# Reordering the side work of a chunked linear-attention loop (adaLN block with a mixture of experts, one Trainium2 core)

## The chip, the cores and the metric

The kernel runs on one core of a Trainium2 chip. The metric is device time in microseconds (us), as the median of several runs. The engines are PE (TensorE), DVE (VectorE), ACT (ScalarE) and POOL (GpSimd); SP issues DMAs. All of them run their own instruction streams and wait for one another through semaphores.

## What is computed

An adaLN transformer block on x of shape (4, 2048, 256), all in fp32: causal linear attention with 16 heads of 16, then a router that sends each token to two of eight experts.

```python
mod = (silu(c) @ wmod).reshape(4, 6, 1, -1)
sa, ca, ga, sb, cb, gb = ...            # ga, gb pushed away from zero
h = layernorm(x) * (1 + ca) + sa
q, k, v = phi(h @ wq.T), phi(h @ wk.T), h @ wv.T      # phi(a) = elu(a) + 1
# per head, over t:  S += k_t v_t^T ;  z += k_t
#                    out_t = (S^T q_t) / max(z . q_t, 1e-6)
x = x + ga * (out @ w_out.T)
h = layernorm(x) * (1 + cb) + sb
gates = softmax(h @ w_router.T); top 2; at most 1280 tokens an expert
x = x + gb * sum_e combine_e * (silu(h @ w_gate.T) @ w_down[e].T)
```

## The kernel before

Tokens are taken in groups of G = 512 (16 groups, `g`), and each group in NT = 4 chunks of 128 tokens (`j`). The kernel has three stages: a setup with a preamble for the first groups, the token loop (`for s in range((NG + 2) * NT)`, L743), and the expert stage from L827 on. The expert stage isn't touched by the change.

**One chunk of the token loop.** `scores` (L406) computes the in-chunk scores on PE into the PSUM tile `psc` (one buffer), and DVE masks them in two operations `at` (L419). A chunk later `attend` (L457) multiplies the masked scores with the values into `po`, ACT copies it to `oT` (L472), and `project_out` (L475, through `done()`) multiplies `oT` with the gated output weights `wob`, and DVE adds the result `pw` to x and takes its statistics (L485, L260). `keep_state` (L428) adds the chunk's key-value product `pst` to `s_acc` on DVE, and POOL masks it into `s_msk` (L444); `from_state` (L447) uses that state at the end of the next chunk. So `psc` of a chunk can start only when both `at` of the chunk before are done.

**Side work.** Around this fixed part, each chunk carries pieces of three other groups:

- for the next group (`nxt` = g+1): `project` for k and q (L303: PE, then ACT exp and relu, then one DVE operation), `values` (L319), `keys_by_token` (L338, PE transposes that ACT copies to `kk`), `running_keys` (L352, a DVE scan `zc` for each half h), `times_keys` (L365, the POOL product `zq`), `denominators` (L371: PE sums `zq` into `pd`, DVE computes `den` and `rden`), `scaled_q` (L387: PE spreads `rden` into `pr`, DVE computes `qs`, ACT computes `qeo`);
- for the group after it (`nrm` = g+2): the first layer norm (`stats`, `spread_of`, `normalise` to `xna` on ACT) and `to_features` (transposes `pta` on PE, `hTa` on ACT); the input tile itself is loaded for g+3;
- for groups behind: `prv` = g-1 has its second norm (`xnm`), `to_features` (`ptm`, `hTm`), `logits`, `ranks` (softmax and top 2 on DVE), `row_inputs` (POOL, two products a chunk of rows into `hrow`); `old` = g-2 has `dispatch` (PE positions `pp`, fourteen small DVE operations, the last of them `idx`) and `send` (POOL issues two indirect DMAs for each of the four row tiles, `slots<-hrow,idx`).

**PSUM.** Everything that isn't `psc`, `po` or `pst` goes through `bank()` (L75), a pool of two tiles: the third bank asked for waits until the first was read out.

```python
    ps = ctx.enter_context(tc.tile_pool(name="ps", bufs=2, space=PSUM))
    def bank(name):
        return ps.tile([P, 512], F32, tag="bank", name=name)
```

**What sets the order.** The instructions of PE, ACT and DVE stand in program order (L721); POOL's are placed by a scheduler, which in the steady state puts most of the eight `send` DMAs of a group early in the group.

```python
    with tc.manual_schedule(engines={ET.PE, ET.Activation, ET.DVE}):
```

In one steady group the banks follow each other on PE as: k0, pw(3), k1, q0, pp | q1, pw(0), v0 | pd, v2, pw(1), ptm0, ptm1, pr0, pr1 | pl, kk0, kk2, pw(2), pta0, pta1, lt, with `|` between chunks.

SP's queue holds the loads of x, the zero-fill of the 10,240 row slots (L617, eight DMAs in each of ten early chunks) and the writes of x to the output (L495).

## Time and profile before

| | |
|---|---|
| median of 3 runs | 1087.3 us (1087.07 to 1090.0) |
| the profiled execution | 1088.37 us, its span 1086.7 us |
| token loop, from the first `psc` to the first expert transposes | 67.3 to 759.5 us of the span |
| write of x of groups 0, 1, 2, 3 issued at | 107.0, 144.6, 180.5, 222.1 us |
| the same for groups 4 to 12 | 264.2, 307.4, 349.6, 392.2, 434.4, 477.8, 520.0, 562.7, 605.0 us |
| the same for groups 13, 14, 15 | 648.4, 689.2, 716.8 us |

How to read it: the write of a group's x is issued when its last chunk was added, some 7 us into the next group, so the differences are the group periods. The page of the profile gives busy time and counts for each engine and the costliest groups of instructions, "idle before" being the time its engine stood still ahead of them and what ended that. A line `L419 DVE TENSOR_TENSOR at<-psc,tri ... x128` reads: source line, engine, operation, output from inputs, count. PEld is PE's weight load, which overlaps with PE. PEclk is the granted share of PE's clock.

### The profile page before, as it was taken

To read this page: it belongs to the slowest core of one execution; us is meant where nothing else is said; L and a number is where in the kernel's file an instruction comes from. 1 tells how busy PE (TensorE), PEld (TensorE's weight loads), DVE (VectorE), ACT (ScalarE), POOL (GpSimd) and SP (SyncE) were. 2 spreads that over 40 slices of the span, in tenths; PEclk is the share of its full clock that TensorE was granted. 3 is DMA by queue.
4 is the path that set the end of the run, shared out by engine and by line. 5 is a ranking of instruction groups with operands and counts; after the bars stand their busy time and mean duration, and the time that the engine had idled before them with its cause. 6 is when DMAs were issued, how large, how long until landed. Compare 5 with 4: busy or idle time off the path is not lost.

```text
span 1086.7 us, 17841 instructions
## 1 busy us (share of the span) xinstructions
PE 915.0 (84%) x6832; PEld 642.5 (59%) x6832; DVE 626.7 (58%) x1448; ACT 363.2 (33%) x722; POOL 563.1 (52%) x690
## 2 busy tenths in 40 slices
PE   5879989879779888897897798740999999999996
PEld 4547756656656656566565576620566666666664
DVE  3546887676685676676766856742334444434443
ACT  0344534425434344344254343210221221222221
POOL 3122565664844746636638547554535445445553
PEclk9989999899899899899899999955999999999998
DMA  5006766221221212202201100022544444344321
GB/s 193 1 1 235 266 227 245 99 99 40 100 72 68 99 50 70 93 35 66 75 33 51 37 30 14 29 78 68 198 138 137 142 162 147 125 160 161 112 68 49
DMA packets 62901, 110.68 MB, mean 102 GB/s; under 512 B 9934, under 2 KB 30670, under 8 KB 62816
## 3 DMA queue, kind: packets, MB, share of 16 engines
q1 hardware_dynamic: 39040, 59.71, 16.7%
q0 software_dynamic: 17920, 42.48, 11.2%
q10 hardware_dynamic: 5856, 7.35, 2.0%
q8 instruction: 54, 0.88, 0.3%
q14 instruction: 31, 0.25, 0.1%
HBM read 47.69 MB, written 74.68 MB: 113 GB/s over the span
## 4 chain that ended last, share of the span: by engine, by line
PE 49%; issue 14%; POOL 13%; DVE 10%; ACT 7%; DMA 5%; SPq 0%; POOLq 0%; DVEq 0%; ACTq 0%
PE pe L695 9%; POOL slots L625 7%; PE ph L681 7%; PE pk L310 5%; DMA rows<-slots 4%; PE pv L325 4%; PE pw L484 3%; PE psc L413 3%; PE po L464 3%; PE pst L434 3%; PE pr L395 3%; PE pq L310 2%; POOL zq L369 2%; PE po L452 1%; POOL s_msk L444 1%
## 5 line engine op out<-in xcount | busy, mean ns | idle before, releaser
L625 POOL DMA_INDIRECT slots<-hrow,idx x128 | 144.5, 1129 | 68.3 <-DVE idx L610 28.4
L695 PE MATMUL pe<-wd,hid 128*128 128x256 f32 x640 | 158.9, 385 | 11.6 <-DVE hid L690 8.7
L419 DVE TENSOR_TENSOR at<-psc,tri 128x1024 f32<-128x1024 f32 x128 | 150.0, 1213 | 23.4 <-PE psc L413 23.3
L681 PE MATMUL ph<-hTe,wg_sb 128*128 128x512 f32 (+1 forms) x384 | 153.3, 526 | 0.7 <-issue 0.7
L695 PEld LDWEIGHTS pe<-wd,hid 128*128 128x128 f32 x640 | 116.0, 189 | 56.5 <-DVE y L702 14.7
L707 POOL DMA_INDIRECT out_dram<-y,tok x80 | 78.6, 982 | 98.0 <-DVE y L706 54.6
L659 POOL DMA_INDIRECT xc<-out_dram,tok x80 | 81.2, 1015 | 68.7 <-issue 44.3
L689 ACT ACTIVATE th<-ph 128x512 f32<-128x512 f32 (+1 forms) x96 | 50.5, 526 | 190.8 <-PE ph L681 134.2
L681 PEld LDWEIGHTS ph<-hTe,wg_sb 128*128 128x128 f32 x384 | 70.6, 191 | 45.0 <-issue 31.8
L690 DVE SCALAR_TENSOR_TENSOR hid<-th,ph 128x512 f32<-128x512 f32 (+1 forms) x96 | 57.0, 596 | 62.4 <-ACT th L689 46.3
L702 DVE SCALAR_TENSOR_TENSOR y<-pe,rows 128x256 f32<-128x256 f32 x80 | 38.6, 483 | 87.4 <-PE pe L695 58.7
L413 PE MATMUL psc<-qeo,k 32*128 32x256 f32 x1024 | 74.3, 404 | 16.0 <-DVE at L419 16.0
L325 PE MATMUL pv<-wqkv_sb,hTa 128*128 128x256 f32 x256 | 79.3, 466 | 5.0 <-ACT req L316 4.7
L444 POOL TENSOR_TENSOR s_msk<-s_acc,bd 128x256 f32<-128x256 f32 x60 | 50.6, 843 | 60.5 <-DVE s_acc L442 46.9
L484 PE MATMUL pw<-wob,oT 128*128 128x256 f32 x256 | 71.2, 402 | 5.9 <-ACT kk L350 2.6
L325 PEld LDWEIGHTS pv<-wqkv_sb,hTa 128*128 128x128 f32 x256 | 58.6, 240 | 20.9 <-ACT req L316 11.0
L464 PE MATMUL po<-at,vpad 128*32 128x128 f32 x2048 | 70.6, 278 | 0.2 <-issue 0.2
L484 PEld LDWEIGHTS pw<-wob,oT 128*128 128x128 f32 x256 | 50.0, 202 | 30.5 <-issue 15.7
L485 DVE TENSOR_TENSOR x<-x,pw 128x256 f32<-128x256 f32 x64 | 26.6, 416 | 71.6 <-PE pw L484 71.6
L310 PE MATMUL pk<-hTa,wqkv_sb 128*128 128x512 f32 x128 | 62.9, 617 | 4.8 <-ACT rek L316 4.4
L464 PEld LDWEIGHTS po<-at,vpad 128*32 128x32 f32 x2048 | 52.8, 110 | 21.9 <-issue 21.6
L413 PEld LDWEIGHTS psc<-qeo,k 32*128 32x128 f32 x1024 | 46.7, 186 | 26.9 <-DVE at L419 18.9
(147 smaller groups left out, 1518.5 us busy)
## 6 DMA issues: line engine op xcount, KB each, us to landing
slots<-free SPq DMA_DIRECT2D x80, 262.0 KB
rows<-slots SPq DMA_DIRECT2D x16, 1048.0 KB
x<-in_x_dram SPq DMA_DIRECT2D x16, 512.0 KB
out_dram<-x SPq DMA_DIRECT2D x16, 512.0 KB
rows<-slots SPq DMA_DIRECT2D x8, 524.0 KB
wd<-in_wdT_dram ACTq DMA_DIRECT2D x8, 512.0 KB
slots<-hrow,idx POOLq DMA_INDIRECT x128
wmod_sb<-in_wmod_dram ACTq DMA_DIRECT2D x1, 1536.0 KB
```

Source lines behind the costliest of these rows:

```text
L310: nc.tensor.matmul(pq, wqkv_sb[:, k, o + h * P : o + (h + 1) * P], hT[:, k, :], start=(k == 0), stop=(k == NH - 1))
L325: nc.tensor.matmul(pv[:, i * D : (i + 1) * D], hT[:, k, (j + i) * P : (j + i + 1) * P], wqkv_sb[:, k, 2 * D : 3 * D], start=(k == 0), stop ...
L413: nc.tensor.matmul(psc[:, a, h], kT[r : r + 32, h, cols], qeo[r : r + 32, h, :, cols], start=True, stop=True,)
L419: masked = nc.vector.tensor_tensor(at, psc[:, 2 * m : 2 * m + 2].rearrange("p i h q t -> p (i h q) t"), tri.unsqueeze(1).to_broadcast([P, ...
L444: nc.gpsimd.tensor_tensor(s_msk, s_acc, bd.unsqueeze(1).to_broadcast([P, NH, P]), ALU.mult)
L464: nc.tensor.matmul(po[32 * a : 32 * a + 32, h * P : (h + 1) * P], vp[:, j, h * 4 + a, q : q + 2, :], att[a // 2][:, a % 2, h, q, :], start ...
L484: nc.tensor.matmul(pw[:, :D], oT[:, h, :], G_["wob"][:, h, :], start=(h == 0), stop=(h == NH - 1))
L625: row = nc.gpsimd.indirect_dma_start(out=slots[:, :], out_offset=bass.IndirectOffsetOnAxis(ap=idx[:, c, j : j + 1], axis=0), in_=hr[:, j, ...
L659: got = nc.gpsimd.indirect_dma_start(out=xc[:, i + j, :], out_offset=None, in_=out[:, :], in_offset=bass.IndirectOffsetOnAxis(ap=tok[:, j ...
L681: nc.tensor.matmul(ph[:, :m], wg_sb[:, k, f * P : (f + 1) * P], hT[:, k, :m], start=(k == 0), stop=(k == NH - 1),)
L695: nc.tensor.matmul(pe[:, j, :], hid[:, f, j * P : (j + 1) * P], wds[e][:, f, :], start=(f == 0), stop=(f == NF - 1),)
L707: put = nc.gpsimd.indirect_dma_start(out=out[:, :], out_offset=bass.IndirectOffsetOnAxis(ap=tok[:, j : j + 1], axis=0), in_=y[:, j, :], in ...
```

## The change

The changed kernel does the same operations on the same shapes. Only one kind is added: the routed positions `pp` are copied from PSUM to an SBUF tile `pos` by ACT, and `dispatch` reads `pos`. The rest is moved:

- POOL joins the engines with a fixed order. `send` is issued four DMAs at a time in chunks 2 and 3 (before: in each chunk), `row_inputs` in the same two chunks; `zq` is issued directly after the scan of its half.
- k is projected a group further ahead: in chunk 3 for g+2 (before: in chunk 0 for g+1). The transposes `pta` that it needs move from chunk 3 to chunk 2.
- q stands in chunk 0 (both halves), `keys_by_token` in chunk 1 (before: chunk 3), both `values` in chunk 1, `dispatch` in chunk 1 (before: chunk 0).
- The first norm of g+2 is applied (`xna`) in chunk 0 (before: chunk 2); its statistics are taken a group earlier, for g+3 in chunk 2 (before: for g+2 in chunk 1). The load of g+3 stays in chunk 1.
- `nmr` (shift of the norm) becomes a function of its own, `shift_of`, issued earlier than `normalise`; `wob` has two buffers and is made ahead; the constants of `hrow` are written with row 0.
- The preamble also takes the statistics of group 2 and projects k of group 1.

The banks of a steady group now follow as: q0, pw(3), q1 | kk0, kk2, pw(0), v0, v2, pp | pd, pta0, pta1, pw(1), ptm0, ptm1, pr0, pr1 | pl, k0, pw(2), k1, lt. On ACT, chunks 0 and 1 are: oT(3), exp and relu of q0 and q1, four `xna`, oT(0), two kk copies, four `vpad` copies, four `xnm`, `pos`, oT(1). On DVE, chunk 1 is: two `at`, `s_acc`, x, statistics, scan of half 1, `dispatch`; chunk 2 begins with the next two `at`, `den`, `rden`.

The diff, without context that says nothing:

```diff
@@ -272,12 +272,16 @@
         nc.gpsimd.tensor_tensor(rstd, ve, mhalf, ALU.pow)
         G_["mr", which] = mv, rstd
 
+    def shift_of(g, which):
+        mv, rstd = G_.pop(("mr", which))
+        nmr = small.tile([P, NT], F32, tag=f"nmr{which}", name=f"nmr{which}_{g}")
+        nc.vector.scalar_tensor_tensor(nmr, mv[:, :, 0], -1.0, rstd, ALU.mult, ALU.mult)
+        G_["ns", which] = nmr, rstd
+
     def normalise(g, which, src):
 
         n = f"{which}_{g}"
-        mv, rstd = G_.pop(("mr", which))
-        nmr = small.tile([P, NT], F32, tag=f"nmr{which}", name=f"nmr{n}")
-        nc.vector.scalar_tensor_tensor(nmr, mv[:, :, 0], -1.0, rstd, ALU.mult, ALU.mult)
+        nmr, rstd = G_.pop(("ns", which))
         xn = w1.tile([P, NT, D], F32, tag=f"xn{which}", name=f"xn{n}")
         for j in range(NT):
             nc.scalar.activation(
@@ -349,24 +353,20 @@
                     )
             nc.scalar.copy(kk[:, j : j + 2].rearrange("p j h s -> p (j h s)"), pk)
 
-    def running_keys(g):
+    def running_keys(g, hs):
 
         kT = G_["k", g]
-        zc = w2.tile([P, NH, G], F32, tag="zc", name=f"zc_{g}")
-        for h in range(NH):
+        if 0 in hs:
+            G_["zc", g] = w2.tile([P, NH, G], F32, tag="zc", name=f"zc_{g}")
+            G_["zq", g] = w1.tile([P, NH, G], F32, tag="zq", name=f"zq_{g}")
+        zc = G_["zc", g]
+        for h in hs:
             nc.vector.tensor_tensor_scan(
                 zc[:, h, :], ones_g, kT[:, h, :],
                 0.0 if g % GPB == 0 else G_["zc", g - 1][:, h, G - 1 : G],
                 ALU.mult, ALU.add,
             )
-        G_["zc", g] = zc
-        G_.pop(("zc", g - 1), None)
-
-    def times_keys(g, h):
-
-        if h == 0:
-            G_["zq", g] = w1.tile([P, NH, G], F32, tag="zq", name=f"zq_{g}")
-        nc.gpsimd.tensor_tensor(G_["zq", g][:, h, :], G_["zc", g][:, h, :], G_["q", g][:, h, :], ALU.mult)
+            nc.gpsimd.tensor_tensor(G_["zq", g][:, h, :], zc[:, h, :], G_["q", g][:, h, :], ALU.mult)
 
     def denominators(g):
 
@@ -472,38 +472,33 @@
         nc.scalar.copy(oT.rearrange("p h t -> p (h t)"), po[:, : NH * P])
         G_["oT", g, j] = oT
 
+    def gated_out(b):
+
+        wob = G_["wob", b] = w2.tile([P, NH, D], F32, tag="wob", name=f"wob_{b}")
+        for h in range(NH):
+            nc.gpsimd.tensor_tensor(wob[:, h, :], wout_sb[:, h, :], gab[:, b, 0, :], ALU.mult)
+
     def project_out(g, j):
-        b = g // GPB
-        if g % GPB == 0 and j == 0:
-            wob = G_["wob"] = w1.tile([P, NH, D], F32, tag="wob", name=f"wob_{g}")
-            for h in range(NH):
-                nc.gpsimd.tensor_tensor(wob[:, h, :], wout_sb[:, h, :], gab[:, b, 0, :], ALU.mult)
-        oT, xt = G_.pop(("oT", g, j)), xs[g]
+        wob, oT, xt = G_["wob", g // GPB], G_.pop(("oT", g, j)), xs[g]
         pw = bank(f"pw_{g}_{j}")
         for h in range(NH):
-            nc.tensor.matmul(pw[:, :D], oT[:, h, :], G_["wob"][:, h, :], start=(h == 0), stop=(h == NH - 1))
+            nc.tensor.matmul(pw[:, :D], oT[:, h, :], wob[:, h, :], start=(h == 0), stop=(h == NH - 1))
         nc.vector.tensor_tensor(xt[:, j, :], xt[:, j, :], pw[:, :D], ALU.add)
         stats(g, "m", j, xt)
 
 
     to_slots, added = [], []
 
-    def second_norm(g):
-
-        b = g // GPB
-        xt = xs[g]
-        added.append(nc.sync.dma_start(og[g], xt))
-        hr = hrows[g % 2]
-        if g % GPB < 2:
-            nc.gpsimd.tensor_copy(
-                hr[:, :, O_GB : O_GB + D], gab[:, b, 1, :].unsqueeze(1).to_broadcast([P, NT, D])
-            )
-        nc.gpsimd.tensor_scalar(hr[:, :, O_TOK], tok0, float(g * G), None, ALU.add)
-
     def row_inputs(g, j):
 
-        b = g // GPB
-        h2 = hrows[g % 2][:, j, :D]
+        b, hr = g // GPB, hrows[g % 2]
+        if j == 0:
+            if g % GPB < 2:
+                nc.gpsimd.tensor_copy(
+                    hr[:, :, O_GB : O_GB + D], gab[:, b, 1, :].unsqueeze(1).to_broadcast([P, NT, D])
+                )
+            nc.gpsimd.tensor_scalar(hr[:, :, O_TOK], tok0, float(g * G), None, ALU.add)
+        h2 = hr[:, j, :D]
         nc.gpsimd.tensor_tensor(h2, G_["xm", g][:, j, :], scb[:, b, 1, :], ALU.mult)
         nc.gpsimd.tensor_tensor(h2, h2, scb[:, b, 0, :], ALU.add)
 
@@ -566,21 +561,27 @@
         state["cnt"] = cnt
         G_["route", g] = gt_, mask, rank, cnt
 
-    def dispatch(g):
-
-        gt_, mask, rank, cnt = G_.pop(("route", g))
-        hr = hrows[g % 2]
-
-        def wide(t):
-            return t.unsqueeze(2).to_broadcast([P, NT, NE])
-
-        pp = bank(f"pp_{g}")
+    def positions(g):
+        gt_, mask, rank, cnt = G_["route", g]
+        pp = G_["pp"] = bank(f"pp_{g}")
         nc.tensor.matmul(
             pp[:, : NT * NE], tri, mask.rearrange("p j e -> p (j e)"), start=True, stop=False
         )
         nc.tensor.matmul(
             pp[:, : NT * NE], ones, cnt[:, :NT, :].rearrange("p j e -> p (j e)"), start=False, stop=True
         )
+        pos = small.tile([P, NT * NE], F32, tag="pos", name=f"pos_{g}")
+        nc.scalar.copy(pos, pp[:, : NT * NE])
+        G_["pos"] = pos
+
+    def dispatch(g):
+
+        gt_, mask, rank, cnt = G_.pop(("route", g))
+        hr, pp = hrows[g % 2], G_.pop("pos")
+
+        def wide(t):
+            return t.unsqueeze(2).to_broadcast([P, NT, NE])
+
         flat = gt_.rearrange("p j e -> p (j e)")
 
         slot = small.tile([P, NT, NE], F32, tag="slot", name=f"slot_{g}")
@@ -718,21 +719,24 @@
     NG = N // G
     ET = mybir.EngineType
 
-    with tc.manual_schedule(engines={ET.PE, ET.Activation, ET.DVE}):
-        for g in range(2):
+    with tc.manual_schedule(engines={ET.PE, ET.Activation, ET.DVE, ET.Pool}):
+        gated_out(0)
+        for g in range(3):
+            if g == 1:
+                load_x(2)
             for j in range(NT):
                 stats(g, "a", j, xs[g])
             spread_of(g, "a")
-            normalise(g, "a", xs[g])
-            to_features(g, "a", 0)
+            if g < 2:
+                shift_of(g, "a")
+                normalise(g, "a", xs[g])
+                to_features(g, "a", 0)
+                for h in range(NH):
+                    project(g, "k", h, D, 2)
             if g == 0:
-                load_x(2)
-                for h in range(NH):
-                    project(0, "k", h, D, 2)
-                running_keys(0)
                 for h in range(NH):
                     project(0, "q", h, 0, 1)
-                    times_keys(0, h)
+                running_keys(0, (0, 1))
                 values(0, 0)
                 values(0, 2)
                 denominators(0)
@@ -744,6 +748,7 @@
             g, j = divmod(s, NT)
             nxt = g + 1 if g + 1 < NG else None
             nrm = g + 2 if g + 2 < NG else None
+            far = g + 3 if g + 3 < NG else None
             prv = g - 1 if 0 <= g - 1 < NG else None
             old = g - 2 if g >= 2 else None
 
@@ -751,7 +756,7 @@
                 if last is not None:
                     project_out(*last)
                     if last[1] == NT - 1:
-                        second_norm(last[0])
+                        added.append(nc.sync.dma_start(og[last[0]], xs[last[0]]))
 
             if g < NG:
                 masked = scores(g, j)
@@ -765,60 +770,65 @@
                 logits(prv)
             if g < NG and not (g % GPB == GPB - 1 and j == NT - 1):
                 keep_state(g, j)
+            for i in {2: (0, 1), 3: (2, 3)}.get(j, ()):
+                if old is not None:
+                    send(old, i)
+            for i in {2: (0, 1), 3: (2, 3)}.get(j, ()):
+                if prv is not None:
+                    row_inputs(prv, i)
             if j == 0:
                 if nxt is not None:
-                    project(nxt, "k", 0, D, 2)
+                    project(nxt, "q", 0, 0, 1)
+                done()
+                if prv is not None:
+                    spread_of(prv, "m")
+                if nxt is not None:
+                    project(nxt, "q", 1, 0, 1)
+                    running_keys(nxt, (0,))
+                if nrm is not None:
+                    shift_of(nrm, "a")
+                    normalise(nrm, "a", xs[nrm])
+                if prv is not None:
+                    shift_of(prv, "m")
+            elif j == 1:
+                if nxt is not None:
+                    keys_by_token(nxt)
                 done()
                 if nxt is not None:
-                    project(nxt, "k", 1, D, 2)
-                    project(nxt, "q", 0, 0, 1)
-                if prv is not None:
-                    spread_of(prv, "m")
-                if old is not None:
-                    dispatch(old)
-                if nxt is not None:
-                    running_keys(nxt)
-                    times_keys(nxt, 0)
-            elif j == 1:
-                if nxt is not None:
-                    project(nxt, "q", 1, 0, 1)
-                    times_keys(nxt, 1)
+                    running_keys(nxt, (1,))
+                    values(nxt, 0)
+                    values(nxt, 2)
                 if prv is not None:
                     normalise(prv, "m", xs[prv])
                     G_["xm", prv] = G_["xnm", prv]
-                done()
-                if nxt is not None:
-                    values(nxt, 0)
+                    xs.pop(prv)
+                if old is not None:
+                    positions(old)
+                    dispatch(old)
+                if far is not None:
+                    load_x(far)
+            elif j == 2:
                 if nrm is not None:
-                    for i in range(NT):
-                        stats(nrm, "a", i, xs[nrm])
-                    spread_of(nrm, "a")
-                if g + 3 < NG:
-                    load_x(g + 3)
-            elif j == 2:
-                if nxt is not None:
-                    values(nxt, 2)
+                    to_features(nrm, "a", 0)
                 done()
                 if prv is not None:
                     to_features(prv, "m", 2)
-                if nrm is not None:
-                    normalise(nrm, "a", xs[nrm])
                 if nxt is not None:
                     scaled_q(nxt)
+                if far is not None:
+                    for i in range(NT):
+                        stats(far, "a", i, xs[far])
+                    spread_of(far, "a")
             else:
-                if nxt is not None:
-                    keys_by_token(nxt)
+                if nrm is not None:
+                    project(nrm, "k", 0, D, 2)
                 done()
                 if nrm is not None:
-                    to_features(nrm, "a", 0)
+                    project(nrm, "k", 1, D, 2)
+                if g % GPB == GPB - 1 and g + 1 < NG:
+                    gated_out(g // GPB + 1)
                 if prv is not None:
                     ranks(prv)
-                    xs.pop(prv)
-            if old is not None:
-                send(old, j)
-            if prv is not None and j >= 1:
-                for i in {1: (0,), 2: (1, 2), 3: (3,)}[j]:
-                    row_inputs(prv, i)
             last = None
             if g < NG:
                 from_state(g, j)
```

## The prediction

> **What bounds the kernel now.** I read the page first (engine totals, slices), then the waits, then one steady group in the timeline, then stretches of it with the granted clock.
>
> ```profile
> PE 915.0 (84%) x6832; PEld 642.5 (59%) x6832; DVE 626.7 (58%) x1448; ACT 363.2 (33%) x722; POOL 563.1 (52%) x690
> ...
> PEclk9989999899899899899899999955999999999998
> ```
>
> PE is the busiest engine, but in the token loop the clock line dips once a group. The waits name the stall behind it:
>
> ```profile
> PEld pd L377 <- POOL zq L369: 51.7, 14, 4.2
> PE pd L377 <- POOL zq L369: 47.9, 14, 3.9
> ```
>
> The timeline of group 7 shows its cause and cost:
>
> ```profile
> 357.19 2.33 DVE L357 TENSOR_TENSOR_SCAN zc<-ones_g,k 128x512 f32<-128x512 f32 x2
> ...
> 365.13 0.97 POOL L625 DMA_INDIRECT slots<-hrow,idx  x1 [0.30 <-issue]
> ...
> 366.79 1.29 POOL L369 TENSOR_TENSOR zq<-zc,q 128x512 f32<-128x512 f32 x1
> ...
> 368.14 0.65 PE L377 MATMUL pd<-zq,hpick 128*32 128x128 f32 x8 [3.94 <-POOL zq L369]
> ...
> 369.74 3.62 PE L325 MATMUL pv<-wqkv_sb,hTa 128*128 128x256 f32 x8
> ```
>
> The second `zq` stands behind four sends on POOL; PE waits 3.94 us, and afterwards runs cold: the `pv` that takes 1.83 us from start to next start in chunk 1 (358.56 to 360.39) takes 3.41 here (369.74 to 373.15). The stretches agree:
>
> ```profile
> 364.00:368.10 4.10, 0.20 (x8) 0.00 (x0) 3.57 (x10) 1.77 (x5) 3.77 (x4) 0.87 0.70 205
> 368.10:371.50 3.40, 3.36 (x17) 2.62 (x18) 1.58 (x3) 0.00 (x0) 3.23 (x5) 0.50 0.58 224
> 371.50:374.90 3.40, 3.40 (x13) 2.66 (x11) 0.32 (x1) 0.65 (x2) 3.21 (x4) 0.65 0.14 55
> ```
>
> Groups 3 to 12 take (605.0 - 180.5)/10 = 42.45 us each; groups 1 and 2, without the stall and at clock 1.00, 37.6 and 35.9. Half clock lasts 3.4 and 6.8 us in turn, which costs half of that, 2.56 us on average. So before is 36 us of work, some 3.9 of stall, some 2.6 of cold clock. DVE is busy 29.7 us of such a group (stretch 307.4 to 349.6), so it has little slack once PE no longer stalls.
>
> **What the Trainium skill says.** "TensorE: Matmul & The Clock Gate", Part 1: PE drops to half clock after an idle window of about 3.4 us, windows run free, and a busy window restores it. The trace agrees (0.50 above) and is stricter: going through its windows, one with PE idle for 57% of it was already followed by half clock. A stall of some 2 us or more can therefore trigger it. The same page, "Architectural detail", calls ACT and DVE strict FIFOs; the trace agrees: at 362.81 `xnm` runs its 2.08 us on ACT while `pv`, done at 360.39, waits behind it for its copies. "Perfetto Trace Analysis", Optimizing Tensor Performance, asks that matmul groups rotate through PSUM banks so that the evacuation of one hides under the next; with two banks, a third group waits for the first one's reader, and that is where the new order gets into trouble.
>
> **The change part by part.** *The `zq` wait.* `zq` now follows its scan on POOL (1.29 us) and comes a chunk before `pd`. The 3.9 us stall and its cold clock go: up to 6.4 us a group.
>
> *What is late next.* I laid one group of the new order out with durations from the timeline above, warm clock, taking A = start of the first `at` on DVE. Each step is the latest of what it waits for:
>
> 1. DVE chunk 0: two `at` 2.26, `s_acc` 0.35, q0 0.6, x 0.45, statistics 0.43, aggregates 0.41, `ve` 0.25, q1 0.6, scan 1.1, `nmra` 0.4: A+6.85.
> 2. ACT has the four `xna` ahead of oT(0) and kk. They need `nmra`: 2.08, then oT 0.37, kk 0.55: A+9.85. `pw`(0) needs oT(0) and the bank of kk0, so PE stands there. PE itself got there at A+6.6 (the next psc starts 4.85 before A; +1.08, attend 1.02, pst 0.55, q 1.75, pw 0.86, q1 1.98 with its wait, po 0.45, psc 1.08, attend 1.02, pst 0.55, kk 1.1). First new stall: 3.25 us.
> 3. PE `pw` 0.86, v0 1.73, v2 1.73: A+14.2.
> 4. ACT v copies 0.65, `xnm` 2.08 (moved ahead of it), `pos` 0.2: A+17.1. `pos` isn't in the trace; the 128x32 ACT row of gates is 0.23. Bounds 0.15 to 0.3.
> 5. DVE has been free since A+12.75 and can't go past `dispatch`: 4.35 us of wait. Dispatch 2.98, the next two `at` 2.3, `den` 0.3: A+22.7. Queued behind it are these `at`, and PE's chunk.
> 6. PE went on (pp 0.35, po 0.45, psc, attend, pd 0.4, pst, pta0 0.55) to A+18.65; `pta1` needs the bank of `pd`, which `den` frees. Second new stall: 4.1 us.
> 7. PE pta1 0.55, pw 0.86, ptm 1.1 and pr 1.8 with 0.35 of waiting for ACT: A+27.35. (DVE's qs, the statistics of g+3 and the `at` end at A+32.3, not last.)
> 8. PE po 0.45, psc 1.08, attend 1.02, pl 0.5, pst 0.6, k0 1.72: A+32.7; ACT exp and relu 1.08, PE k1 1.75, ACT 1.1: A+36.7.
> 9. DVE k1 0.68, ranks 3.7 (342.32 to 346.04): next A at A+41.05.
>
> A cold clock comes on top. Where the window boundaries fall decides: after the first stall the loss on steps 3 is 0 to 3 us, after the second 1.4 to 3 us on step 7. Followed through successive groups it settles near 1.7 + 1.6, a period of 13 windows (44.4 us; before is 12.5 windows). So a steady group goes from 42.45 to 44.4, +1.95.
>
> *Other groups.* Group 2 already has dispatch and late ranks in it: 35.9 to some 44, +8. Group 1: no dispatch, PE-bound, -1.5. Group 13 lacks the statistics of g+3: -1. Group 14 lacks `xna`, `pta` and the k projection: 40.8 to some 33, -8. Group 15 loses a POOL wait (4.55 us of PE at 710.58 for `s_msk` behind sends) as POOL's fixed order puts `s_msk` first: -4.
>
> *Preamble.* k of group 1 (two cold projections, exp, relu, DVE) and the statistics of group 2 now stand before the first psc, +5.5; the first group has that much less to wait for, +4 net.
>
> *Drain.* Sends of group 14 start after `xnm` 2.08, `pos` and dispatch instead of before: the first at 4.5 us after the last x addition (716.32 to 720.87), now some 8; POOL is serial from there: +3.5.
>
> *At nothing:* `wob` ahead (8 x 0.73 on POOL, busy 25 of 42 us), `shift_of` (same instruction; its `rstd` is there in time), the order of sends (SP and POOL queues: `s_msk` stands before each block of four sends, and is needed a chunk later; 4 x 1.28 fits in). Cover gone, they would cost PE 1 to 4 us a group. The x load is issued after `xnm`, at A+16.9, and before took at most 6.4 us (364.9 issue to the last packet at 371.3); its reader is at A+28: 5 us of slack.
>
> Sum: 4 - 1.5 + 8 + 10 x 1.95 - 1 - 8 - 4 + 3.5 = +20.5 us on the profiled 1088.4: 1109. That execution lies 1.1 us above the median of the runs, within their spread.
>
> **Rivals.** *N, not slower:* the two stalls stand, but don't trip the clock (place: the windows at `pw`(0) and `pta1`; price 3.3 us a group). Then a group takes 41.05: 10 x (41.05 - 42.45) = -14, group 2 +5, the rest as above -7: 1072. It decides from where each stall leaves less than half of a window idle, for which both would need to be under 2 us or be split by a boundary. Against it: 3.25 and 4.1 us; all twelve such stalls of groups 3 to 14 tripped it.
> *F, faster:* the chain isn't closed because DVE isn't late at A (it is by 4.85 us, mostly from ranks). Then both stalls shrink under 2 us and PE's own 34 to 37 us bound: 10 x (37 - 42.45) = -54, others about -4: 1030. For it: PE's sum of work above is 33.7. Against it: DVE has 29.7 us of work a group and two forced waits.
> *L, slower by more:* the load of g+3 lands late, or both stalls cost two cold windows (DMA share was 0.6 to 0.7 while sends ran). With 47 us a group 1135, with 48 some 1145.
>
> **How the numbers follow.** Forecast 0.62 (own range 1090 to 1128), N 0.13, F 0.12, L 0.13. Predicted: 1109. The range leaves out F and the upper part of L: 1058 to 1140. A measurement here tells 0.3% (3.3 us) from no change. Faster: F, N and a corner of the forecast, 0.26; same 0.05; slower 0.69.
>
> **What would show it.** Right: no `pd` wait on `zq`; a PE wait at `pw` for ACT kk of about 3 us and one at `pta` for DVE `den` of about 4, thirteen times each; a DVE wait at `slot` for ACT `pos` of about 4; clock dips twice a group. Wrong: ACT reaching oT(0) before PE (no wait at `pw`), ranks ending before the next psc, or PE at clock 1.00 through the loop; then F or N holds.

## The result, and the profile after

The changed kernel takes 1145.6 us (median of 4 runs, 1140.5 to 1148.1) against 1087.7 before: ratio 1.052, 95% interval 1.048 to 1.056. Forecast were 1109, with a range to 1140: the direction is right, the time is 37 us longer than forecast. The profiled execution spans 1142.3 us at a mean granted clock of 0.919 (before 1086.7 us at 0.939).

First the clock, from the slices of the page after (tenths of full speed, 40 slices):

```profile
PEclk9989999799898998998989889785699999999999
```

The token loop lies in slices 3 to 27, and from the eighth on every second or third is below 9. Read stretch by stretch, the granted clock falls to half twice in each of groups 3 to 13, mostly for 3.41 us each time. Next the table of waits after (who, for whom: us in all, times, longest us):

```profile
DVE slot L589 <- ACT pos L574: 85.5, 15, 15.8
...
PE pw L485 <- ACT kk L354: 40.8, 15, 3.3
...
PE pw L485 <- DVE den L382: 24.3, 11, 2.2
...
ACT oT L472 <- remote: 9.9, 2, 5.8
...
DVE nmrm L278 <- POOL rstdm L272: 9.3, 3, 6.7
```

The wait of `pd` for `zq` is gone, as forecast. In its place are the three waits that the prediction named: PE at `pw` for the `kk` copies, DVE at `slot` for `pos`, PE for `den`. The last two lines were not foreseen: ACT waits for something the profile doesn't show ("remote"; the kernel before has twelve such waits, of at most 1.4 us), and group 3 waits for `rstdm`.

The timeline after, in a steady group whose first `at` starts at A = 516.03 (start, duration, engine; in brackets the idle time before, and who ended it):

```profile
522.54 2.07 ACT L287 ACTIVATE xna<-x,nmra,rstda 128x256 f32<-128x256 f32 x4 [2.78 <-POOL rstdm L272]
...
525.40 1.13 PE L485 MATMUL pw<-wob,oT 128*128 128x256 f32 x4 [2.77 <-ACT kk L354]
...
526.37 5.30 PE L329 MATMUL pv<-wqkv_sb,hTa 128*128 128x256 f32 x16
...
532.24 2.08 ACT L287 ACTIVATE xnm<-x,nmrm,rstdm 128x256 f32<-128x256 f32 x4
...
534.22 0.17 ACT L574 COPY pos<-pp 128x32 f32<-128x32 f32 x1
...
534.42 0.18 DVE L589 TENSOR_SCALAR slot<-pos 128x32 f32<-128x32 f32 x1 [5.78 <-ACT pos L574]
...
537.32 2.35 DVE L419 TENSOR_TENSOR at<-psc,tri 128x1024 f32<-128x1024 f32 x2
```

Read from the top: ACT spends 2.07 us on `xna`, and PE stands 2.77 us at `pw`(0), at A+9.4, for the `kk` copy queued behind it. Then `pv` takes 5.30 us, the most of it on half a clock (0.51 from 526.6 to 530.0), where step 3 has 3.46 for v0 and v2 together. `xnm` stands ahead of `pos`, DVE waits 5.78 us at `slot`, the next two `at` come only then, and PE waits again, 2.22 us for `den`. The second stall sits at `pw`(1) and not at `pta1`: the bank of `pd` went to `pw`(1).

The time of the whole run by parts, counted from the first `at` of each group in the two traces (us; the last column is an experiment told below):

| part | before | forecast | after | `row_inputs` early |
|---|---|---|---|---|
| to the first `at` of group 1 | 99.6 | +4 | +10.4 | +12.0 |
| group 1 | 37.6 | -1.5 | +2.6 | +4.2 |
| group 2 | 39.6 | +8 | +3.1 | +4.8 |
| groups 3 to 12 | 424.5 | +19.5 | +35.3 | +13.3 |
| group 13 | 43.5 | -1 | +2.3 | -1.5 |
| group 14 | 41.3 | -8 | -6.3 | -6.8 |
| group 15, to the last x addition | 30.2 | -4 | +4.3 | -2.7 |
| from there to the end | 370.3 | +3.5 | +3.9 | +1.4 |
| sum | 1086.7 | +20.5 | +55.6 | +24.7 |

Group 3 alone went from 41.6 to 50.9 us, groups 4 to 12 from 42.55 to 45.44 each.

### The profile page after: what moved, and what is told of

The parts are those of the page before. It is cut to its first block, busy times and chain, and to the rows that moved or that the text cites. A ratio compares the mean times of both kernels' runs of the same rounds, so it can differ in the third digit from the quotient of the medians.

```text
span 1142.3 us, 17805 instructions
## 1 busy us (share of the span) xinstructions
PE 937.3 (82%) x6832; PEld 663.5 (58%) x6832; DVE 635.7 (56%) x1448; ACT 366.9 (32%) x738; POOL 557.2 (49%) x690
## 4 chain that ended last, share of the span: by engine, by line
PE 36%; DVE 18%; issue 15%; ACT 9%; POOL 6%; DMA 4%; SPq 1%; another core or an unknown queue 1%; POOLq 0%; DVEq 0%; ACTq 0%
PE pe L696 6%; DVE at L419 5%; PE pv L329 5%; PE ph L682 5%; PE pk L314 4%; PE pw L485 4%; PE pr L395 3%; DMA rows<-slots 2%; ACT xna L287 2%; ACT xnm L287 2%; POOL slots L626 2%; PE ptm L300 2%; PE psc L413 2%; PE po L464 2%; POOL out_dram L708 1%
## 5 line engine op out<-in xcount | busy, mean ns | idle before, releaser
L626 POOL DMA_INDIRECT slots<-hrow,idx x128 | 129.4, 1011 | 53.7 <-issue 42.8
L485 PE MATMUL pw<-wob,oT 128*128 128x256 f32 x256 | 86.2, 469 | 77.5 <-ACT kk L354 40.8
L485 PEld LDWEIGHTS pw<-wob,oT 128*128 128x128 f32 x256 | 53.3, 222 | 105.3 <-ACT kk L354 34.0
L660 POOL DMA_INDIRECT xc<-out_dram,tok x80 | 80.9, 1011 | 67.2 <-issue 42.5
L691 DVE SCALAR_TENSOR_TENSOR hid<-th,ph 128x512 f32<-128x512 f32 (+1 forms) x96 | 57.0, 595 | 61.9 <-ACT th L690 50.9
L329 PE MATMUL pv<-wqkv_sb,hTa 128*128 128x256 f32 x256 | 76.3, 464 | 3.7 <-DVE x L486 3.7
L369 POOL TENSOR_TENSOR zq<-zc,q 128x512 f32<-128x512 f32 x32 | 41.4, 1293 | 66.4 <-DVE zc L364 58.1
L464 PE MATMUL po<-at,vpad 128*32 128x128 f32 x2048 | 73.0, 280 | 0.5 <-issue 0.4
L329 PEld LDWEIGHTS pv<-wqkv_sb,hTa 128*128 128x128 f32 x256 | 61.9, 242 | 17.4 <-DVE x L486 4.5
L314 PE MATMUL pk<-hTa,wqkv_sb 128*128 128x512 f32 x128 | 65.8, 642 | 4.8 <-ACT rek L320 4.1
L314 PE MATMUL pq<-hTa,wqkv_sb 128*128 128x512 f32 x128 | 61.5, 605 | 3.8 <-ACT req L320 3.7
```

What stands on the lines that cost most here:

```text
L314: nc.tensor.matmul(pq, wqkv_sb[:, k, o + h * P : o + (h + 1) * P], hT[:, k, :], start=(k == 0), stop=(k == NH - 1))
L329: nc.tensor.matmul(pv[:, i * D : (i + 1) * D], hT[:, k, (j + i) * P : (j + i + 1) * P], wqkv_sb[:, k, 2 * D : 3 * D], start=(k == 0), stop ...
L464: nc.tensor.matmul(po[32 * a : 32 * a + 32, h * P : (h + 1) * P], vp[:, j, h * 4 + a, q : q + 2, :], att[a // 2][:, a % 2, h, q, :], start ...
L485: nc.tensor.matmul(pw[:, :D], oT[:, h, :], wob[:, h, :], start=(h == 0), stop=(h == NH - 1))
L626: row = nc.gpsimd.indirect_dma_start(out=slots[:, :], out_offset=bass.IndirectOffsetOnAxis(ap=idx[:, c, j : j + 1], axis=0), in_=hr[:, j, ...
L660: got = nc.gpsimd.indirect_dma_start(out=xc[:, i + j, :], out_offset=None, in_=out[:, :], in_offset=bass.IndirectOffsetOnAxis(ap=tok[:, j ...
```

## The experiments

Times are medians; ratios are against runs of the kernel before on the same chip, with their 95% interval. Theory Q at the outset: the change loses by two waits of PE behind unrelated work in ACT's order, each of which also trips the clock. Rivals: D, DVE's own work bounds the group; P, POOL's fixed order is what costs.

**1. Undo the two places in ACT's order.** One run sets the positions ahead of the second norm, one sets `xna` behind everything in chunk 1, one does both.

```diff
 # first: in chunk 1                      # second: from chunk 0 to the end of chunk 1
+                positions(old)
                 normalise(prv, "m", xs[prv])
-                positions(old)
                 dispatch(old)
+                normalise(nrm, "a", xs[nrm])
```

> The changed kernel with `positions` ahead of the second norm in chunk 1, so that ACT copies `pos` before the four `xnm` (2.08 us). Theory Q (the loss is two waits behind unrelated ACT work, each of which also trips the PE clock): the DVE wait at `slot` falls by about 2 us, the PE stall behind `den` falls from about 3.1 us to about 1 us and no longer trips the clock; 3.8 us in each of some 12 groups: 1100 us (1085 to 1120). Rival D (DVE's own work sets the period, the waits only fill slack): within 5 us of 1145. Rival P (POOL's fixed order with blocks of four sends is the loss): also within 5 us of 1145.

> The changed kernel with the four `xna` moved from chunk 0 to the end of chunk 1 on ACT, behind oT, kk, v copies, `xnm` and `pos`. Theory Q: the PE wait at `pw` for ACT kk (about 2.8 us, 15 times) and the clock dip behind it go, 4.5 to 5 us a group: 1085 us (1065 to 1110). Rivals D and P: within 5 us of 1145.

> Both moves at once. Theory Q: neither stall is left over 2 us, the clock stays at 1.00 in the steady groups, a group takes 37 to 39 us: 1050 us (1025 to 1080), so faster than the kernel before. Rivals D and P: within 8 us of 1145.

Measured: 1101.7 (1.014, 1.010 to 1.017), 1093.8 (1.005, 1.004 to 1.007) and together 1067.2 (0.980, 0.977 to 0.983). Groups 4 to 12 take 42.0, 41.1 and 39.4 us each (45.4 as changed). With `xna` late PE's wait for `kk` falls from 40.8 us to 3.9; with both moves, what is left of the other two is

```profile
DVE slot L589 <- ACT pos L574: 33.4, 14, 13.4
...
PE pta L300 <- DVE den L382: 14.3, 12, 1.2
```

DVE does the same work in all of these, so D falls: 78 of the 110 us that will turn out to be the price of the moves lie in the place of two pieces of ACT work. The three came 2, 9 and 17 us above what was expected; experiment 6 tells what was still in the way.

**2. POOL's order alone.** The kernel before, with POOL in program order; then with `wob` a batch ahead in two buffers as well.

```diff
-    with tc.manual_schedule(engines={ET.PE, ET.Activation, ET.DVE}):
+    with tc.manual_schedule(engines={ET.PE, ET.Activation, ET.DVE, ET.Pool}):
+        gated_out(0)                      # second kernel; next batch in chunk 3
```

> The kernel before with one edit: POOL also in program order, so that both `zq` stand ahead of the sends of their chunk. If the 6.4 us a group that I gave the `pd` wait and its cold clock are right: groups 3 to 14 fall from 42.4 to 36 to 37.5 us: 1022 us (1005 to 1050). Rival: the fixed POOL order costs as much elsewhere (sends waiting for the zero-fill, `s_msk` behind sends): 1070 to 1095.

> The kernel before with POOL in program order, and the gated output weights `wob` made one batch ahead in a second buffer, as in the change; nothing else of the change. If the 46 us of groups 4, 8 and 12 come from `wob` standing behind the sends in POOL's fixed order (PE's wait for `wob`: four times, 34.1 us in all), that wait goes, the three groups fall to the 38.5 us of their neighbours, and the time is about 1042 us (1035 to 1052), the fastest so far. Rival: those groups are long because the first group of each batch has other work in it as well (the rows of `gab` into `hrow`); then `wob` leaves the wait list but another takes its place and the time stays at 1060 to 1070 us.

Measured: 1067.5 (0.983, 0.980 to 0.986), then 1035.7 (0.952, 0.950 to 0.954), the fastest kernel of the study and faster than both given ones. The first gained 20 us, a third of what was expected; its table of waits says why:

```profile
PE pw L484 <- POOL wob L480: 34.1, 4, 9.5
...
PE pd L377 <- POOL zq L369: 14.5, 11, 1.4
```

`wob` was late four times: for 5.5 us in group 0, where `zq` stood ahead of it, and for 9.5 us each in groups 4, 8 and 12 (46 us each), behind `zq`, sends and `s_msk`. With it made ahead, groups 4 to 12 take 38.1 us, and the clock of that kernel's page has no dip left in the steady groups:

```profile
PEclk9989999999999999999999999857999999999999
```

So the change contains a gain of 52 us, POOL's order with `wob` ahead, and loses 110 through its other moves. P as "POOL's order costs" is wrong for the kernel before. For the changed one it was asked directly, on both bases:

```diff
-    with tc.manual_schedule(engines={ET.PE, ET.Activation, ET.DVE, ET.Pool}):
+    with tc.manual_schedule(engines={ET.PE, ET.Activation, ET.DVE}):
```

> The changed kernel with POOL's order left to the scheduler again, all else as changed. Theory Q (the change loses by two stalls of PE behind ACT and DVE, each followed by a half clock): only the excess of group 3 goes, where `rstdm` stands behind the sends (50.8 us against 45.4 of the groups after it), some 6 us, and PE's waits at `pw` for `kk` (40.8 us) and DVE's at `slot` for `pos` (85.5 us) stay: 1138 us (1128 to 1148). Rival P (POOL's fixed order with sends in blocks of four is what costs): 40 us or more come back, 1105 us or less.

> The changed kernel with the positions ahead of the second norm, and the first norm moved behind them (the two moves of the run that gave 1067.2), and POOL's order left to the scheduler. Theory Q: the excess of group 3 (48.2 us against 38 to 41 of the others) goes as well, about 1059 us (1052 to 1066). Rival P': by now POOL's order is what holds the steady groups, then 1045 us or less; and if the scheduler places the sends ahead of `s_msk`, PE waits at the end of each chunk and it is 1070 us or more.

Measured: 1155.3 (1.062, 1.059 to 1.064) and 1123.5 (1.032, 1.029 to 1.034). Both expectations failed: on the base with both moves undone, the scheduler's order costs 56 us. The second one had an arm for 1070 us or more, but for PE waiting for `s_msk`, and that wait is 0.2 us in all. See experiment 5.

**3. Does the low clock have a price?** The changed kernel with nine unused matmuls a group added where PE stalls.

```diff
+        for _ in range({1: 5, 2: 4}.get(j, 0)):
+            nc.tensor.matmul(pst[:, 256:512], ident, wqkv_sb[:, 0, :256], start=True, stop=True)
```

> The changed kernel with work added and none taken away: five further 128x256 matmuls on PE at the end of chunk 1 and four at the end of chunk 2, into the unused half of `pst`, which no one reads. They stand just ahead of or beside the two stalls, so that PE is active in those windows. Theory Q with the clock as a price of its own: the half-clock windows after the stalls go or become fewer, each worth up to 1.7 us; with about 3.3 us a group over ten groups, 1108 us (1095 to 1125) in spite of some 10 us a run of added matmul time. Rival: the low clock only falls into time that is waited for anyway, so it has no price, and the added matmuls make it 1145 us or more.

Measured: 1134.2 (1.041, 1.038 to 1.044), granted clock 0.950 instead of 0.919, groups 4 to 12 at 43.6 instead of 45.4 us. PE's busy time rose from 937.3 to 965.7 us, and the kernel was 11 us faster: the dips have a price of their own. Not all of them went, and the gain is a third of what was expected.

**4. Group 3, the preamble, and parts of the change alone.** The zero-fill twice as dense; k of group 1 in the loop instead of the preamble; and, on the kernel of 1035.7 us, the sends in blocks, then `dispatch` in chunk 1 behind `xnm`.

```diff
-                if 2 <= s < TPE + 2: free_slots(s - 2, masked)        # zero-fill
+                for i in (2 * s - 4, 2 * s - 3): ...
+                for h in range(NH if s == 0 else 0): project(1, "k", h, D, 2)   # k of group 1
-            if old is not None: send(old, j)                           # blocks
+            for i in {2: (0, 1), 3: (2, 3)}.get(j, ()): send(old, i)
```

> The changed kernel with the zero-fill of the row slots issued twice as densely: sixteen DMAs in each of five chunks from chunk 2 of group 0 on, where it is eight in each of ten. Theory Z: group 3 is 5 us longer than its neighbours because the first block of sends (POOL, 181.05 us) waits for a zero-fill that ends in the middle of group 2, and `rstdm` stands behind the sends; with the fill over a group earlier that excess goes, group 3 falls from 50.9 to about 46 us, and the time to about 1141 us (1136 to 1146). Rival: POOL issues the sends of group 2 late because `idx` and the blocks of chunks 2 and 3 are late in themselves; group 3 stays at 50 us and the time at 1146 us or, as the denser fill holds up the loads of x, above.

> The changed kernel with k of group 1 projected in chunk 0 of group 0, ahead of q, and not in the preamble; every other k stays a group ahead. Theory: the 10.3 us that the preamble and group 0 lose are mostly these two projections, which run on a cold clock behind a PE that waited for `xna` (6.01 us at 67.86); the first `psc` moves from 73.8 to 68 us, the two projections cost 3.6 us warm in chunk 0, and the write of group 0's x comes at about 113 us instead of 117.3: 1141 us (1137 to 1146). Rival: the loss is in group 0's own stalls (2.4 us at `pw` for `kk`, the `at` behind statistics of group 2), so the write stays at 117 us and the time at 1146.

> The fastest kernel so far (the one before with POOL in program order and `wob` a batch ahead, 1035.7 us), and to it one more part of the change alone: the sends in blocks of four in chunks 2 and 3, the row inputs behind them, and the constants of `hrow` with row 0. Theory: in a steady group blocks of sends cost nothing, as `s_msk` stands ahead of them: groups 4 to 12 stay at 37.4 to 38.5 us. If the excess of group 3 in the changed kernel is the blocks' (Z), group 3 grows from 37.8 to 43 us or more here, and the time is 1041 us (1036 to 1048). Rival P'': results of PE that come while POOL issues a block arrive late (2.7 us was seen behind a pair, 4.6 behind a block of four), and each steady group grows by 1 to 3 us: 1048 to 1070 us.

> The kernel with the sends in blocks, and one more part of the change: `dispatch` moves from chunk 0 to chunk 1, behind the second norm, and reads the positions through ACT's copy `pos`. Everything else on ACT and PE keeps the old order. Theory Q: the move is dear in the changed kernel only since ACT reaches `xnm` and `pos` late there, behind four `xna`, oT(0), kk and v; here ACT ends `xnm` about when DVE gets to `slot` (348.9 and 349.6 us in the run of 1035.7), so a group grows by at most 1.5 us: 1036 to 1058 us, say 1046. Rival D': it is the 3 us of DVE work itself, set ahead of the next `at` and `den`, that costs; then PE waits for `den` as in the changed kernel and a group grows by 4 us or more: 1078 us or above.

*Zero-fill:* 1143.6 (1.056, 1.052 to 1.060), no different from the changed kernel. Group 3 falls to 45.3 us as expected, but the denser fill holds up a load of x (a 13.7 us wait of DVE), and group 1 takes 53.4. *k of group 1:* 1132.2 (1.045, 1.041 to 1.049). The first `at` comes 5.3 us earlier and group 0 takes 5.8 us more: the rival of that expectation was right, and its gain comes later (group 3 -3.5, groups 4 to 12 -0.5 each, group 15 -5.3), which nothing in the edit explains. *Blocks of sends:* 1043.8 (0.963, 0.959 to 0.967); steady groups 38.2 us, group 3 from 37.8 to 43.7 us between its writes of x (40.0 to 48.0 from `at` to `at`), as expected. *`dispatch` in chunk 1:* 1053.9 (0.971, 0.966 to 0.975), beside the last one +10.1 us, 0.9 a group, within the range expected. That move is cheap where ACT reaches `pos` in time: Q holds and D' falls.

**5. What the sends do to PE.** In the kernel with both moves undone and POOL left to the scheduler, DVE waits for "remote" twelve times, 32.8 us. Its timeline there:

```profile
532.20 1.15 PE L413 MATMUL psc<-qeo,k 32*128 32x256 f32 x16
532.24 0.97 POOL L626 DMA_INDIRECT slots<-hrow,idx  x1 [0.30 <-issue]
...
533.28 0.73 PE L464 MATMUL po<-at,vpad 128*32 128x128 f32 x17
533.52 0.97 POOL L626 DMA_INDIRECT slots<-hrow,idx  x1 [0.30 <-DMA slots<-hrow,idx]
...
535.41 1.02 POOL L626 DMA_INDIRECT slots<-hrow,idx  x1 [0.17 <-issue]
...
535.67 0.30 PE L464 MATMUL po<-at,vpad 128*32 128x128 f32 x2 [1.13 <-issue]
...
537.23 2.36 DVE L419 TENSOR_TENSOR at<-psc,tri 128x1024 f32<-128x1024 f32 x2 [2.61 <-remote]
```

The last matmul of `psc` ends at 533.4 in the trace, `at` starts at 537.2, and in between POOL issues sends. PE itself is held up as well: the 32 matmuls of `po` that follow come in pieces and take 4.66 us, where 1.08 is usual; in each of groups 3 to 14 one such set takes 3.3 to 5.5 us. The ends of matmuls are modelled in the trace, so it can't tell whether PE's results are late or PE's work is. A late result stands in group 15 of the changed kernel too:

```profile
730.61 1.08 PE L464 MATMUL po<-at,vpad 128*32 128x128 f32 x32
...
733.14 0.97 POOL L626 DMA_INDIRECT slots<-hrow,idx  x1 [0.30 <-issue]
...
734.41 0.97 POOL L626 DMA_INDIRECT slots<-hrow,idx  x1 [0.31 <-issue]
...
736.35 0.37 ACT L472 COPY oT<-po 128x256 f32<-128x256 f32 x1 [5.81 <-remote]
```

ACT's `oT` waits 5.81 us for a `po` that PE had done at 731.7; it starts 1 us after the fourth send was issued, and PE stands 4.44 us behind it. The sends were left out of both kernels, and then, in the changed one, replaced by plain DMAs of the same rows on SP, to fixed places.

```diff
-        for c in range(2):                # left out
+        for c in range(0):
-            row = nc.gpsimd.indirect_dma_start(...)                    # plain
+            row = nc.sync.dma_start(slots[at : at + P, :], hr[:, j, :])
```

> The changed kernel with the sends left out (no row goes into the slots, so the expert stage works on the rows of the zero-fill); all else as changed. Theory H: while POOL issues sends, PE's results reach the other engines late. Then ACT's wait for `remote` at oT in group 15 (5.8 us, PE's at `pw` behind it 4.4) goes, with the wait of group 3 for `rstdm` behind the sends (6.7) and the sends' own tail after the last group (some 4): 1128 us (1118 to 1136); PE's waits for `kk` and `den` and DVE's for `pos` stay as they are. Rival T: the late results of PE have nothing to do with the sends; then only `rstdm` and the tail are saved, 1136 us, and the 5.8 us wait stays.

> The kernel with both moves on ACT undone and POOL's order left to the scheduler (1123.5 us; 1067.2 with POOL in program order), with the sends left out (the expert stage works on the rows of the zero-fill). Theory H: what POOL's order costs there, some 5 us a group, is the five sends in one block beside the third chunk, which hold back PE's result for `at` (DVE's wait for `remote` 12 times, 32.8 us): without sends that wait is under 5 us in all, groups 4 to 12 fall from 44.4 to 40 us, 1067 us (1050 to 1085). Rival T: the scheduler's order is bad for another reason (`s_msk` or `rstda` late); then the groups stay above 43 us and the time above 1100.

> The changed kernel with each send as a plain DMA of the same 128 rows on SP's queue, to rows that are fixed instead of routed (so a row stands at another place, and rows of groups 10 to 15 overwrite others): the same bytes at the same point of the order, but nothing for POOL to issue. If it is POOL's issuing of indirect DMAs that holds back PE's results (H1), the wait of 5.8 us in group 15 goes as it does without sends, and the time is within 6 us of the run without sends. If it is the traffic of the rows (H2), the wait stays at 3 us or more and the time within 6 us of the changed kernel, 1145.

Measured: 1068.4 (0.981, 0.974 to 0.988), 1028.5 (0.946, 0.943 to 0.948) and 1082.4 (0.998, 0.996 to 1.000). The token loop has no wait for "remote" left in any of the three. In the second kernel the groups fall from 44.5 to 40.4 us, no `po` takes more than 1.74 us, and `ranks` has the same length with and without the sends, so the 4.1 us a group are the hold's, in line with H. The plain DMAs keep the rows' bytes and have no such wait, which fits H1, but in the changed kernel the wait of group 15 is no test of it: it is also gone with the denser zero-fill, with k of group 1 in the loop, and in experiment 6, where POOL issues all the sends. There (first kernel, 709.8 us) a send is issued while `po` ends at 709.95, and `oT` starts at 710.07. So no kernel without the sends shows the hold, but a kernel with them need not show it either; that POOL's issuing and not the rows' traffic is what holds PE (H1) is likely, not shown.

The whole times missed what was expected. The changed kernel without sends is 60 us below its 1128, and the plain-DMA kernel is 14 us above that one, where either arm allowed 6. The hold isn't all that an edit takes away: the stretch after the last x addition is 22 to 36 us shorter, in which the last sends are gone or moved and other rows are worked on. But the token loop of the plain-DMA kernel is 40 us shorter too, far more than H gives, and groups 4 to 12 take 43.0 us instead of 45.4.

**6. What the sends displace.** The timeline of the changed kernel, `ranks` in one group:

```profile
466.30 0.98 POOL L626 DMA_INDIRECT slots<-hrow,idx  x1 [0.31 <-issue]
...
467.28 0.75 POOL L502 TENSOR_TENSOR hrow<-xnm,scb 128x256 f32<-128x256 f32 x1
...
467.45 0.87 DVE L543 TENSOR_TENSOR ahead<-gates 128x256 f32<-128x256 f32 x1
...
468.11 0.80 POOL L503 TENSOR_TENSOR hrow<-hrow,scb 128x256 f32<-128x256 f32 x1
...
468.25 0.94 DVE L545 TENSOR_TENSOR tie<-gates 128x256 f32<-128x256 f32 x1
...
469.22 0.83 DVE L546 TENSOR_TENSOR tie<-tie,tri 128x256 f32<-128x256 f32 x1
...
470.09 0.84 DVE L547 TENSOR_TENSOR ahead<-ahead,tie 128x256 f32<-128x256 f32 x1
...
470.96 0.42 DVE L550 TENSOR_REDUCE rank<-ahead 128x32 f32<-128x256 f32 x1
```

Four sends end, then POOL's `row_inputs` products run beside `ranks`, and each DVE operation that takes two inputs from SBUF lasts 0.83 to 0.94 us. `rank`, a reduction of one input, has its 0.42. Over ten groups `ranks` takes 5.14 us from the start of `mx` to that of `mask`, in the kernel before and in the plain-DMA kernel 3.54. Two of the same operations before:

```profile
344.03 0.42 DVE L550 TENSOR_TENSOR tie<-gates 128x256 f32<-128x256 f32 x1
344.48 0.42 DVE L551 TENSOR_TENSOR tie<-tie,tri 128x256 f32<-128x256 f32 x1
```

One edit keeps the sends and moves the products, on the changed kernel and on that with both moves undone:

```diff
+            for i in {2: (0, 1, 2, 3)}.get(j, ()): row_inputs(prv, i)
             for i in {2: (0, 1), 3: (2, 3)}.get(j, ()): send(old, i)
-            for i in {2: (0, 1), 3: (2, 3)}.get(j, ()): row_inputs(prv, i)
```

> The changed kernel with all four `row_inputs` of a group in chunk 2, ahead of the sends, where they stood two in chunk 2 and two in chunk 3, each pair behind four sends. Theory R: in chunk 3 the two pairs of POOL products start when the sends are through, beside `ranks` on DVE, whose operations with two SBUF inputs then take 0.83 to 0.99 us instead of 0.42; `ranks` takes 4.4 to 5.9 us (5.1 in the mean of ten groups) instead of 3.54, and stands at the end of the chain. With the products gone from there every `ranks` takes 3.54 to 3.7 us, a group 1.5 us less: groups 4 to 12 at 43.9 us (43.0 to 44.4), the time 1122 us (1114 to 1130) with what group 3 and 13 gain. Rival: the sends then stand beside `ranks` and hold DVE as much, or the chain ends elsewhere; `ranks` stays above 4.3 us or the groups stay at 45 us: 1140 us or more.

> The kernel with both moves on ACT undone (1067.2 us), and `row_inputs` in chunk 2 ahead of the sends. Theory R: `ranks` there takes 4.4 to 6.0 us, since every group has the pairs beside it; with 3.54 a group falls from 39.4 to 37.7 us and the time to 1046 us (1038 to 1054). Rival: PE's own work of a group (busy 85 to 90%) is the bound by now and the DVE time saved is waited for elsewhere; the groups stay at 39 us and the time at 1062 or above.

Measured: 1115.7 (1.029, 1.027 to 1.031) and 1036.9 (0.956, 0.954 to 0.958). Groups 4 to 12 take 43.92 us, where 43.9 was expected, and 37.57, where 37.7 was; the times are 6 and 9 us below what was expected, the second just outside its range, since other groups gained too. The timeline of `ranks` in the first of them:

```profile
459.45 0.97 POOL L626 DMA_INDIRECT slots<-hrow,idx  x1 [0.30 <-issue]
459.49 0.42 DVE L543 TENSOR_TENSOR ahead<-gates 128x256 f32<-128x256 f32 x1
459.83 0.42 DVE L545 TENSOR_TENSOR tie<-gates 128x256 f32<-128x256 f32 x1
...
460.29 0.42 DVE L546 TENSOR_TENSOR tie<-tie,tri 128x256 f32<-128x256 f32 x1
...
460.72 0.97 POOL L626 DMA_INDIRECT slots<-hrow,idx  x1 [0.30 <-issue]
...
460.74 0.44 DVE L547 TENSOR_TENSOR ahead<-ahead,tie 128x256 f32<-128x256 f32 x1
...
461.21 0.42 DVE L550 TENSOR_REDUCE rank<-ahead 128x32 f32<-128x256 f32 x1
```

Sends now stand beside `ranks`, and its operations take 0.42 to 0.44 us again. It is the products, not the sends, that slow these operations. The Trainium skill has this in "SBUF — State Buffer", Who interferes with whom: a DVE instruction with two SBUF inputs contends with a GpSimd instruction that reads SBUF, and the one that comes second waits. These lines agree, and so does `at`, which reads one of its inputs from PSUM: in the changed kernel each takes 1.21 to 1.23 us, the 60 that run beside such a product as well as the others.

Group 3 fell from 50.9 to 42.5 us by the same edit. In the timeline of the changed kernel the queue there was

```profile
199.99 0.74 POOL L502 TENSOR_TENSOR hrow<-xnm,scb 128x256 f32<-128x256 f32 x1
...
204.92 1.04 POOL L272 TENSOR_TENSOR rstdm<-vem,mhalf 128x4 f32<-128x4 f32 x1
...
206.00 1.23 DVE L278 SCALAR_TENSOR_TENSOR nmrm<-mvm,rstdm 128x4 f32<-128x4 f32 x1 [6.75 <-POOL rstdm L272]
```

with two pairs of products, `cnt` and `s_msk` between the late sends and `rstdm`, for which DVE stood 6.75 us. The late zero-fill sets this off: with the denser fill this wait of DVE is gone and group 3 takes 45.3 us. With the products moved, the wait shrinks to 3.98 us and the excess of group 3 is gone as well.

The second kernel is as fast as that of 1035.7 us within half a per cent, with shorter steady groups (37.57 against 38.09) and a longer start (107.8 us against 98.9 to the first `at` of group 1). What then remains of the moves gains half a microsecond a group and loses it again at the start.

## Why the prediction was right or wrong

**Right: the two stalls, their places and the chain up to its last step.** The prediction has `pw`(0) at A+9.85, and with the cold clock of 1.7 `pos` at A+18.8, `den` at A+24.4 and the last relu of k1 at A+40.0. In the group shown they came at 9.4, 18.4, 23.8 and 39.3. Experiment 1 shows both to be the main loss, experiment 3 that the clock belongs to it. Two dips a group and the new waits came as foretold; that the second stall sits at `pw`(1) makes no difference to the sum.

**Wrong: "At nothing: ... the order of sends".** This is the step that failed. The prediction looked at `s_msk` behind the sends and named a price of 1 to 4 us a group if the cover was gone, but on PE. It didn't ask what else stands behind the sends on POOL: the `row_inputs`, which so come to lie beside `ranks`. Step 9, "ranks 3.7" to the end of `mask`, is the term that was mis-sized by it: 5.3 us counted alike, at the end of the chain, in the mean of ten groups. The table shows the size of it. With only the `row_inputs` moved, the sum of the changes is +24.7 where +20.5 was forecast, and groups 3 to 12, 13, 14, 15 and the end are each within 6.2 us of their terms. The edit is worth 31 us of span, of 35 missing. That the two sums then lie so close is partly luck: the start and group 1 are 14 us over their terms, group 2 and groups 3 to 12 9 us under.

Within that: group 3 (+9.3 where +1.95 was meant) is the same order on POOL, set off by the zero-fill; the blocks alone make 8.0 us of it on another base. Group 15 was to gain 4 us by a wait less, and got another, the 4.4 us of PE behind ACT's 5.8 for the late `po`; the products moved, it gains 2.7.

**Mis-sized: the start, +4, measured +10.4 to the first `at` of group 1, and group 1 itself, +2.6 for -1.5.** The first `at` comes 8.0 us later; the projections of k of group 1 run on a cold clock there (6.0 us at 67.9). The prediction then let group 0 give back part of it, and took group 1 as bound by PE. It priced no stalls there. They are there: with `xna` late, group 0 takes 28.6 us instead of 32.5. Moving the projection doesn't help (experiment 4). It is work of one group paid ahead; group 14 gives 6.3 back.

**Mis-sized, the other way: group 2, +8, measured +3.1.** The 35.9 us that it started from lie between two writes of x, the 44 that it compared with them between two `at`. From `at` to `at` group 2 took 39.6 us before, so that the same 44 was worth +4.4; 3.7 of the 4.9 us are this.

**The `zq` wait, "up to 6.4 us a group".** POOL's order on the kernel before gave 4.45 us a group (42.55 to 38.09), with `wob` made ahead. The term was right in kind and 2 us too high. Rival L's 1145, for 48 us a group, is the measured time, but by luck: groups 4 to 12 took 45.4, no load of x was late, and a stall brought a second cold window only in groups 3, 5, 8 and 12. N and F are out: two stalls trip the clock in each of groups 3 to 13, and the chain closes.

What stays open: by what mechanism, and under which conditions, PE is held while POOL issues sends; what else makes the token loop of the plain-DMA kernel shorter; and why k of group 1 in the loop shortened later groups.

## What to carry to other kernels

When an engine's order is fixed, price every instruction that comes to stand behind a moved block, and ask what then runs beside it on the other engines, not only who waits for it. Two engines that slow each other's reads lose time with no wait in any table: compare the duration of the same instruction, line by line, before and after. And try the parts of a change alone, since here a gain of 52 us lay inside a change that lost 58.

## What the runs showed of the hardware

- While POOL issues a block of indirect DMAs, ACT and DVE can stand for results of PE that the trace has as done, up to 5.8 us behind a block of four, and PE's own matmuls can come in pieces (`po` 3.3 to 5.5 us for 1.08). Without the sends this is gone, but other kernels here issue the same sends and show none of it.
- The 128x256 operations of `ranks` on DVE with two SBUF inputs take 0.83 to 1.00 us instead of 0.42 beside POOL products of two SBUF inputs; `at`, with one input in PSUM, keeps its 1.21 to 1.23.
- Matmuls that no one reads can pay: PE's busy time rose by 28 us and the kernel ran 11 us faster, as the clock dipped less often. The Trainium skill, "TensorE: Matmul & The Clock Gate", Part 1, puts a window of PE activity behind the clock, which fits; but it names an idle window of about 3.4 us, where stalls of 2.2 and 2.8 us, in windows with PE busy for 1.0 and 1.2 of 3.4 us, were enough here.
